# Two transformer layers on one core: row addresses by transposes, pinned engine orders and VectorE additions in the last stage

## The chip, the cores and the metric

The kernel runs on one core of one Trainium2 chip. The metric is the time of one execution in device microseconds (us), as the median of several runs; lower is better. Each profiled execution also has a span, from the first to the last instruction of the core, and the clock that TensorE was granted (1.00 is full speed, 0.50 half). The engines are named as in the profile: PE is TensorE's matmul and PEld its weight load, DVE is VectorE, ACT is ScalarE, POOL is GpSimd, and SP is the engine whose queue issues most DMAs.

## What is computed

Four sequences of 1024 tokens with 256 features pass through two layers, each an attention and a feed-forward part with residual additions. The change touches only the last of the four parts, a routed feed-forward layer in which each of 8 experts picks its best 128 tokens of a sequence:

```python
def _L1_ffn_ref(x, gate_w, experts):
    SINKHORN_ITERS = 8
    ...
    B, N, D = x.shape          # 4, 1024, 256
    E = gate_w.shape[-1]       # 8
    M = N // E                 # 128
    gate_logits = jnp.einsum('bnd,de->bne', x, gate_w)
    competitive_gates = sinkhorn(gate_logits)
    vals, idx = jax.lax.top_k(jnp.swapaxes(competitive_gates, -1, -2), M)
    gate_values = jnp.swapaxes(vals, -1, -2)
    routed_indices = jnp.swapaxes(idx, -1, -2)
    b_idx = jnp.arange(B)[:, None, None]
    routed = x[b_idx, routed_indices]
    routed = jnp.transpose(routed, (2, 0, 1, 3))
    outputs = jnp.einsum('ebmd,edf->ebmf', routed, experts)
    outputs = outputs * jnp.transpose(gate_values, (2, 0, 1))[..., None]
    vals_bmed = jnp.transpose(outputs, (1, 2, 0, 3))
    routed_back = jnp.zeros_like(x).at[b_idx, routed_indices].set(vals_bmed)
    return routed_back
...
x = x + _L1_ffn_ref(_layernorm(x, axis=-1), L1_ffn_gate_w, L1_ffn_experts)
return x
```

Where two experts pick the same token, the later expert's value stands (`set`). So each token gets at most one row of results, that of the highest expert that picked it, and a token picked by none gets zeros.

## The kernel before

The tokens lie as 32 tiles `x_t[i]` of 128 tokens by 256 features; a sequence `b` has `TB` = 8 tiles. The sequences are treated in two groups, `SEQS`: group 0 is sequences 0 to 2, group 1 is sequence 3 alone, since its attention ends last. The code is written as Python generators that emit instructions; a scheduler then orders the instructions of each engine by its own estimate of when each is ready, unless an edge (`tc.issue_after`) pins one behind another. A list `in_turn`, when it is not empty, makes `mm_on` and `turn_on` (matmul and transpose on TensorE, line 82) keep program order; plain `mm` and `nc.tensor.transpose` don't. In the last stage `in_turn` is empty before the change.

The work of the last stage, which lies from about 2085 us to the end:

1. **Column and row sums of the gates** (`share_steps`, lines 1293 to 1324): eight rounds, each a sum over tokens on VectorE (L1305), a product with ones on TensorE (L82) and five short VectorE instructions (L1314 to L1321). Group 0's rounds run in the attention stage; group 1's eight rounds run here.
2. **The choice of tokens** (`choose_parts`): the gates of a group, by expert, are laid out as rows of 1024 tokens; sixteen times VectorE takes the eight largest of each row (`max`) and strikes them out (`match_replace`), all recorded at L1363. After that it looks for their indices (`max_index`, four for each half). Products on TensorE then lay out gate, token and row number of each slot: `slot_gate` (L1410, ScalarE), `slot_tok` and `slot_row` (L1408 and L1409, VectorE). For group 1 this is done in two parts, each after eight rounds. The generator yields between the VectorE instructions, and what is emitted between two yields is what may lie beside them. Inside `choose_parts` these VectorE instructions are already chained to one another.
3. **Gathering the chosen tokens** (`take_rows`, L1420): POOL issues one indirect DMA for each expert and sequence, 128 rows of 1 KB from the DRAM copy `xn_d` into a tile `xg`: 24 for group 0, and four for each part of group 1.
4. **The experts** (`experts_on`, `half_experts`): two tiles at a time are transposed on TensorE (L1436), copied to `xgT` by ScalarE (L1438), multiplied with two experts' weights (L1453, or L1490 for the half tiles of group 1), scaled by the gates on ScalarE into `yg` (L1463, L1499; four buffers) and stored by SP into the DRAM tile `y_d[b]` (L1467, L1503). `experts_on` transposes pair m ahead of the product of pair m - 1.
5. **Signs and ranks** (`signs`, L2133 and L2135): to find out which row of `y_d` belongs to a token, ScalarE makes for each expert a matrix of signs, token number (`place`, a ramp along the columns) against the slot's token (`half_less`), and TensorE multiplies it with a column of slot numbers (`whole_col`, `half_col`). What is accumulated in PSUM (`rank0`, `rank1`) is, for each expert and token, a sum that jumps from one token to the next by the slot's number where the expert has chosen that token. ScalarE copies the sums out (`sums_to`, L2178; `last_sums`, L2241).
6. **Row addresses** (`sources`, L2152 to L2162): for each of the eight tiles, three accumulated products turn the sums of one sequence into a key of 8 numbers per token: expert number, plus 8 times the sum shifted by one token, minus 8 times the sum. VectorE takes the largest of the eight (L2162): the row of `y_d` to be read, or a row of zeros.
7. **Back to the tokens** (`back`, L1511): POOL issues one indirect DMA per tile that reads the 128 rows and **adds** them into `x_t[i]` as it writes (`compute_op=ALU.add`). Then SP stores the tile to the output (`put`, L1521).

In the last stage's body (lines 2165 to 2246) the generators are mixed by counts: sums of group 1 beside experts and signs of group 0, then the choice of group 1 beside the rest of them and beside the addresses of each sequence when its eighth sign is in; then the two halves of sequence 3. The `y_d` rows of a sequence must have landed before its eight reading DMAs are issued.

## Time and profile before

| what | us |
|---|---|
| median of 6 runs (lowest to highest) | 2250.4 (2245.86 to 2258.06) |
| the profiled execution, its own time | 2250.11 |
| its span | 2248.4 |
| PE busy over the span | 2088.1 (93%) |
| DVE, ACT, POOL busy over the span | 1326.9, 1029.1, 641.2 |
| mean granted clock of TensorE over the span | 0.965 |
| group 1's first sum over tokens (L1305) starts | 2089.80 |
| group 1's first `max` (L1363) starts | 2134.64 |
| `slot_row` of group 1's second part ready | 2210.10 |
| last adding gather (L1511) starts | 2241.74 |

The times of the lower rows are microseconds from the start of the span. A line of the timeline gives the start, the duration, the engine, the line of the kernel, the operation, the output and inputs by name (`two`, `acc`, `misc` and `one` are PSUM tiles), the shapes, and how many instructions were merged. In square brackets stands how long the engine was idle before, and what released it; "issue" means that nothing that the profile shows was waited for, and "remote" a signal that the profile can't assign to an instruction. Durations of PE are modelled at their ends, since matmuls are pipelined; a float32 matmul leaves two records.

### The profile page before, as it was taken

Reading aid. Unit: us, or ns where it says so; the run is one execution under the profiler, and the core shown is the slowest. Engines: PE = TensorE matmul, PEld = TensorE weight load, DVE = VectorE, ACT = ScalarE, POOL = GpSimd, SP = SyncE. Lnnn points to the kernel's source line nnn. Section 1 sums busy time; section 2 is a strip of 40 time slices with the busy share of each in tenths; the row PEclk is TensorE's granted clock in tenths of the full one; section 3 lists DMA queues with packets and bytes.
Section 4 is the critical chain, followed back from the end, with each engine's and each line's share of the span. In section 5 each row is a group of like instructions: output and inputs, shape, how many; then the busy total and the mean of one; then the engine's idle time right before and its main releaser. Section 6 shows DMA issues by size and latency. Waiting matters only on the chain. (4 is left out here: it accounts for less than half of the span.)

```text
span 2248.4 us, 50565 instructions
## 1 busy us (share of the span) xinstructions
PE 2088.1 (93%) x20098; PEld 1378.6 (61%) x20098; DVE 1326.9 (59%) x2626; ACT 1029.1 (46%) x1941; POOL 641.2 (29%) x832
## 2 busy tenths in 40 slices
PE   6999989999999999998999999999999999997693
PEld 4777765555788888864555555555555555553472
DVE  6676654522222222245887878778787877898353
ACT  3555542111122222221266666767676766666352
POOL 3656541342000000023421222221221303024454
PEclk9999999999999999999999999999999999997676
DMA  4111106113167667734353222131313131101345
GB/s 147 52 45 48 49 13 200 50 63 136 52 222 237 219 215 233 225 112 103 85 112 68 52 50 61 50 76 49 77 49 77 46 64 42 45 2 55 87 97 119
DMA packets 207303, 212.66 MB, mean 95 GB/s; under 512 B 87208, under 2 KB 167432, under 8 KB 207068
## 3 DMA queue, kind: packets, MB, share of 16 engines
q1 hardware_dynamic: 181788, 169.39, 26.7%
q0 software_dynamic: 14048, 29.67, 5.1%
q10 hardware_dynamic: 11232, 10.37, 1.3%
q8 instruction: 159, 2.61, 0.5%
q14 instruction: 76, 0.62, 0.1%
HBM read 140.64 MB, written 56.92 MB: 88 GB/s over the span
## 5 line engine op out<-in xcount | busy, mean ns | idle before, releaser
L1772 ACT ACTIVATE wide<-one 128x512 f32<-128x512 f32 x1024 | 529.3, 602 | 215.9 <-PE one L86 210.2
L1722 DVE TENSOR_REDUCE tops<-two 128x2 f32<-128x1024 f32 x268 | 326.0, 1218 | 88.0 <-PE two L86 82.2
L1725 DVE TENSOR_REDUCE tops<-one 128x1 f32<-128x512 f32 x488 | 313.4, 680 | 15.2 <-PE one L86 15.2
L86 PE MATMUL acc<-wide,v_t 128*32 128x256 f32 x4096 | 278.7, 389 | 2.6 <-ACT wide L1772 2.1
L86 PE MATMUL two<-xbT,w_t 128*128 128x256 f32 (+1 forms) x1280 | 253.6, 356 | 2.0 <-ACT xbT L1155 1.4
L86 PE MATMUL one<-q_st,k_st 64*128 64x512 f32 x1024 | 238.3, 450 | 2.7 <-ACT wide L1772 1.9
L86 PEld LDWEIGHTS two<-xbT,w_t 128*128 128x128 f32 x1280 | 221.5, 190 | 29.7 <-ACT xbT L1155 1.8
L1188 DVE SCALAR_TENSOR_TENSOR glu_b<-two,b_blk,act_b 128x256 f32<-128x256 f32 (+1 forms) x160 | 72.6, 454 | 244.8 <-ACT act_b L1181 244.8
L86 PE MATMUL one<-top_st,minus 64*128 64x512 f32 x1024 | 209.4, 396 | 0.0
L1181 ACT ACTIVATE act_b<-two,b_blk 128x256 f32<-128x256 f32 (+1 forms) x160 | 72.1, 451 | 295.3 <-PE two L86 136.1
L86 PE MATMUL one<-k_st,q_st 64*128 64x512 f32 x488 | 172.6, 451 | 27.1 <-ACT wide L1772 22.6
L86 PEld LDWEIGHTS acc<-wide,v_t 128*32 128x32 f32 x4096 | 107.7, 109 | 113.7 <-issue 62.4
L289 ACT ACTIVATE act<-two,bT 128x512 f32<-128x512 f32 x60 | 41.2, 687 | 264.9 <-PE two L82 259.4
L86 PEld LDWEIGHTS one<-q_st,k_st 64*128 64x128 f32 x1024 | 101.6, 186 | 92.7 <-ACT wide L1772 39.6
L86 PEld LDWEIGHTS one<-k_st,q_st 64*128 64x128 f32 x488 | 86.8, 184 | 104.9 <-ACT wide L1772 77.7
L86 PE MATMUL acc<-w_t,glu_b 128*128 128x256 f32 x552 | 125.6, 379 | 0.0
L1933 POOL DMA_INDIRECT yr<-ys_d,slot x64 | 61.9, 967 | 211.9 <-DMA ys_d<-yb 80.3
L82 PE MATMUL two<-wide,w_t 128*128 128x512 f32 x256 | 115.1, 603 | 5.6 <-DVE tops L1722 4.9
L1238 POOL TENSOR_TENSOR x<-x,sb_b 128x256 f32<-128x256 f32 x32 | 23.2, 726 | 336.5 <-DVE glu_b L1188 336.5
L619 POOL TENSOR_SCALAR_AFFINE_SELECT pT<-pT 64x512 f32<-64x512 f32 x128 | 84.2, 658 | 114.0 <-ACT pT L609 112.0
L86 PEld LDWEIGHTS acc<-w_t,glu_b 128*128 128x128 f32 x552 | 101.9, 190 | 12.3
L1827 POOL TENSOR_TENSOR y<-y,wide 128x256 f32<-128x256 f32 x32 | 23.3, 730 | 300.7 <-DVE y L1824 235.4
(396 smaller groups left out, 3445.2 us busy)
## 6 DMA issues: line engine op xcount, KB each, us to landing
w_t<-in_L_ffn_rw_dram SPq DMA_DIRECT2D x120, 512.0 KB
halves<-split SPq DMA_DIRECT2D x64, 256.0 KB
q_st<-halves SPq DMA_DIRECT2D x128, 128.0 KB
k_st<-halves SPq DMA_DIRECT2D x256, 64.0 KB
xb<-xs_d SPq DMA_DIRECT2D x31, 256.0 KB
ys_d<-yb ACTq DMA_DIRECT2D x31, 256.0 KB
xs_d<-zeros SPq DMA_DIRECT2D x5, 1536.0 KB
b_t<-in_L_ffn_rb_dram SPq DMA_DIRECT2D x40, 128.0 KB
```

The lines of the kernel that those rows point to most:

```text
L82: return do(*args, **kw)
L86: done = do(*args, **kw)
L289: nc.scalar.activation(act, ps[0], AF.Silu, bias=bT[0][:, f, e : e + 1])
L619: nc.gpsimd.affine_select(out=part, in_=part, compare_op=ALU.is_ge, fill=0.0, base=0, pattern=[[0, 8], [1, WIN]], channel_multiplier=-1,)
L1181: nc.scalar.activation(act[:, :cols], ps[:, ff * cols : (ff + 1) * cols], AF.Silu, bias=b_blk[0][:, f, n : n + 1],)
L1188: nc.vector.scalar_tensor_tensor(glu[:, f, :cols], ps[:, 512 + ff * cols : 512 + (ff + 1) * cols], b_blk[1][:, f, n : n + 1], act[:, :cols ...
L1238: nc.gpsimd.tensor_tensor(x_t[m], x_t[m], sb3_b, ALU.add).ins, newest_glu[0]
L1722: last = nc.vector.tensor_reduce(tops[:, :, j, kk], whole[0], AX.X, ALU.max)
L1725: last = nc.vector.tensor_reduce(tops[:, hh, j, kk : kk + 1], sc[hh], AX.X, ALU.max)
L1772: newest["scalar"] = nc.scalar.activation(pt[:, hh * 512 : (hh + 1) * 512], sc[hh], AF.Exp).ins
L1827: nc.gpsimd.tensor_tensor(y, y, bo_b, ALU.add)
L1933: ga = nc.gpsimd.indirect_dma_start(out=yr[:, :], out_offset=None, in_=ys_d[:, :], in_offset=bass.IndirectOffsetOnAxis(ap=slots[k][:, i : ...
```

## The change

- **Addresses.** The slot columns are scaled by `0.5 * E` instead of 0.5, and the first column of the sums holds minus (expert number plus a constant). Before the first sign of a sequence a product of `place` with `e_part` (expert number / 128 in all 128 rows, two matmuls of 512 columns in float32) adds a ramp of expert number times token number to the accumulated sums. The difference of the sums of two neighbouring tokens then is the whole key. `turned_sums` transposes the sums and the sums shifted by one (16 transposes of 8 by 128 into one PSUM bank), ScalarE copies the first half out (`before`), and VectorE subtracts (`key`) and takes the largest. The products of L2152 and L2154 go, and with them `times_e`.
- **Orders.** `in_line` pins every instruction that passes through it behind the last one of its engine: ScalarE's copies, signs and scalings, VectorE's choice, keys and addresses, and POOL's ramp, gathers and reads. `in_turn` is set, and all TensorE work of the stage goes through `mm_on` and `turn_on`. The body of the stage becomes a written-out order; a pair of experts is transposes, sign, product, sign, two sums, and three steps of the choice. Signs get six buffers. The place of each sum among the pairs is fixed by this order.
- **Additions.** For sequences 2 and 3 the reading DMA no longer adds; it writes a tile `yr`, and VectorE adds it to `x_t[i]`. The stores of sequences 2 and 3 come after the last stores of rows.
- **The tail.** Sequence 3's sums are copied out half by ScalarE and half by VectorE, and the order there is: signs, first transposes, copies of the sums, first pair, the 16 transposes of the sums, second pair, keys.

```diff
@@ -92,6 +92,17 @@
     def turn_on(*args, **kw):
         return on_tensor(nc.tensor.transpose, *args, **kw)
+    lines = {"scalar": [], "vector": [], "gpsimd": []}
+    def in_line(engine: str, do, *args, **kw):
+        with ExitStack() as behind:
+            for ins in lines[engine]:
+                behind.enter_context(tc.issue_after(ins))
+            done = do(*args, **kw)
+        lines[engine][:] = [done.ins]
+        return done
     const = ctx.enter_context(tc.tile_pool(name="const", bufs=1))
...
@@ -1433,9 +1439,9 @@
         for h, xg in enumerate(xgs):
             for kc in range(2):
                 c = (2 * h + kc) * P
-                nc.tensor.transpose(ps[:, c : c + P], xg[:, kc * P : (kc + 1) * P], ident)
+                turn_on(ps[:, c : c + P], xg[:, kc * P : (kc + 1) * P], ident)
         xgT = pool.tile([P, 4, P], F32, tag="xgT", name="xgT", bufs=3)
-        nc.scalar.copy(xgT.rearrange("p k t -> p (k t)"), ps)
+        in_line("scalar", nc.scalar.copy, xgT.rearrange("p k t -> p (k t)"), ps)
...
@@ -1446,48 +1452,39 @@
         slot_gate = chosen[g, 0][0]
-        def product(m: int, xgT):
+        for m in range(0, len(xgs), 2):
+            xgT = turned(xgs[m : m + 2], pool)
+            yield m
             ps = two_banks()
             for h in range(2):
                 for kc in range(2):
-                    mm(
+                    mm_on(
                         ps[:, h * D : (h + 1) * D],
                         lhsT=xgT[:, 2 * h + kc, :],
-                        rhs=w_all[:, (2 * m + h) % E, kc, :],
+                        rhs=w_all[:, (m + h) % E, kc, :],
                         start=(kc == 0),
                         stop=(kc == 1),
                     )
             for h in range(2):
-                b, e = divmod(2 * m + h, E)
+                b, e = divmod(m + h, E)
                 yg = pool.tile([P, D], F32, tag="yg", name="yg", bufs=4)
-                nc.scalar.activation(
+                in_line(
+                    "scalar", nc.scalar.activation,
                     yg, ps[:, h * D : (h + 1) * D], AF.Copy,
-                    scale=slot_gate[:, 2 * m + h : 2 * m + h + 1],
+                    scale=slot_gate[:, m + h : m + h + 1],
                 )
                 nc.sync.dma_start(out=slots_of(SEQS[g][b], e, 0, CAP), in_=yg)
...
             yield m
-    def half_experts(g: int, part: int, m: int, xgs, pool, w_all):
+    def half_experts(g: int, part: int, m: int, xgT, pool, w_all):
...
@@ -1505,16 +1503,22 @@
                     in_=yg[64 * h : 64 * h + 64, :],
                 ).ins
...
+    def backs(b: int, src_row, pool, adds: bool):
+        rows = []
+        for t in range(TB):
+            i = b * TB + t
+            yr = pool.tile([P, D], F32, tag="yr", name="yr", bufs=2 * TB) if adds else x_t[i]
+            in_line(
+                "gpsimd", nc.gpsimd.indirect_dma_start,
+                out=yr[:, :],
+                out_offset=None,
+                in_=y_d[b][:, :],
+                in_offset=bass.IndirectOffsetOnAxis(ap=src_row[:, t : t + 1], axis=0),
+                compute_op=ALU.bypass if adds else ALU.add,
+            )
...
-            whole_col.rearrange("p n e -> p (n e)")[:, :: E + 1], slot_i, 0.5, None, ALU.mult
+            whole_col.rearrange("p n e -> p (n e)")[:, :: E + 1], slot_i, 0.5 * E, None, ALU.mult
         )
         for h in range(2):
...
-        first_sum = -0.5 * (CAP * (CAP + 1) // 2)
+                    half_i[half, part, :], 0.5 * E, None, ALU.mult,
+                )
         n0 = len(SEQS[0])
         sums_to = wpool.tile([32 * (n0 - 1) + E, 1 + S], F32, name="sums_to")
-        nc.gpsimd.memset(sums_to[:, 0:1], first_sum)
         last_sums = wpool.tile([E, 1 + S], F32, name="last_sums")
-        nc.gpsimd.memset(last_sums[:, 0:1], first_sum)
+        e_i = wpool.tile([E, 1], I32, name="e_i")
+        nc.gpsimd.iota(e_i, pattern=[[0, 1]], base=E * CAP * (CAP + 1) // 4, channel_multiplier=1)
+        for rows in [sums_to[32 * b : 32 * b + E] for b in range(n0)] + [last_sums]:
+            nc.gpsimd.tensor_scalar(rows[:, 0:1], e_i, -1.0, None, ALU.mult)
+        e_part = wpool.tile([P, E], F32, name="e_part")
+        nc.gpsimd.tensor_scalar(e_part, expert_no[:, 0], 1.0 / P, None, ALU.mult)
         def half_less(g: int, part: int):
             tok = chosen[g, part][1]
...
@@ -2127,123 +2131,146 @@
             nc.vector.tensor_scalar(less, tok, -1.0, 0.5, ALU.mult, ALU.add)
             return less
...
+        def sign(less, n: int):
+            hot = pool.tile([P, S], BF16, tag="hot", name="hot", bufs=6)
+            in_line("scalar", nc.scalar.activation, hot, place, AF.Sign, bias=less[:, n : n + 1])
+            return hot
+        def halves_on(ps, lhsT, rhs, start: bool, stop: bool):
             for hf in range(2):
-                newest["ranks"] = mm(
+                newest["ranks"] = mm_on(
                     ps[:, hf * 512 : (hf + 1) * 512],
-                    lhsT=col,
-                    rhs=hot[:, hf * 512 : (hf + 1) * 512],
+                    lhsT=lhsT,
+                    rhs=rhs[:, hf * 512 : (hf + 1) * 512],
                     start=start,
                     stop=stop,
                 ).ins
-        def sources(rows, mine):
-
-
+        def turned_sums(rows, mine):
             ps = one_bank()
...
+            for n in range(2):
+                for t in range(TB):
+                    c = (n * TB + t) * E
+                    turn_on(
+                        ps[:, c : c + E], rows[:, t * P + n : (t + 1) * P + n], ident[mine, mine]
                     )
...
+            before = pool.tile([P, TB * E], F32, tag="before", name="before")
+            in_line("scalar", nc.scalar.copy, before, ps[:, : TB * E])
+            return ps, before
+        def sources(ps, before):
+            key = pool.tile([P, TB, E], F32, tag="key", name="key")
+            in_line(
+                "vector", nc.vector.tensor_tensor,
+                key.rearrange("p t e -> p (t e)"), ps[:, TB * E : 2 * TB * E], before, ALU.subtract
+            )
+            src_row = pool.tile([P, TB], I32, tag="src_row", name="src_row")
+            in_line("vector", nc.vector.tensor_reduce, src_row, key, AX.X, ALU.max)
             return src_row
+        in_turn.append("all")
         less0 = half_less(0, 0)
         xgs0 = take_rows(chosen[0, 0], [(n // E, n) for n in range(n0 * E)], pool)
         rank0 = two_banks()
...
+        jobs = experts_on(0, xgs0, pool, w_all)
+        hots, summed = [], iter(range(n0 * E))
+        def one_sign():
+            hots.append(sign(less0, len(hots)))
+        def sum_signs(n: int):
+            for _ in range(n):
+                n = next(summed)
                 b, e = divmod(n, E)
...
+                ps = rank0[32 * b : 32 * b + E]
+                if e == 0 and b:
+                    halves_on(ps, e_part, place, True, False)
+                halves_on(ps, whole_col[:, e, :], hots[n], False, e == E - 1)
+        def ranks(b: int):
             mine = slice(32 * b, 32 * b + E)
...
+            in_line("scalar", nc.scalar.copy, sums_to[mine, 1:], rank0[mine, :])
+            return turned_sums(sums_to[mine], mine)
+        halves_on(rank0[:E], e_part, place, True, False)
         for n, _ in enumerate(share_steps(1, one_bank, 0)):
+            next(jobs)
             if n:
...
+                sum_signs(1)
+            one_sign()
+        choose = choose_parts(1, one_bank, lambda: None, 2)
+        def go_on(n: int):
+            for _ in range(n):
+                next(choose, None)
+        def pair_of_experts():
+            next(jobs)
+            one_sign()
+            next(jobs)
+            one_sign()
+            sum_signs(2)
+            go_on(3)
+        go_on(3)
+        sum_signs(1)
+        at = ranks(0)
+        go_on(1)
+        for _ in range(2):
+            pair_of_experts()
+        backs(0, sources(*at), pool, False)
+        for _ in range(2):
+            pair_of_experts()
+        at = ranks(1)
+        pair_of_experts()
+        go_on(1)
+        backs(1, sources(*at), pool, False)
+        for _ in range(3):
+            pair_of_experts()
         put(0)
-        for _ in sign_job:
-            pass
-        columns = [(NB - 1, m) for m in range(E // 2)]
+        at = ranks(2)
+        while (1, 0) not in chosen:
+            go_on(1)
+        less = half_less(1, 0)
+        xgs = take_rows(chosen[1, 0], [(NB - 1, m) for m in range(E // 2)], pool)
         rank1 = two_banks()[:E]
...
+        halves_on(rank1, e_part, place, True, False)
+        def last_signs(part: int):
+            for m in range(E // 2):
+                halves_on(
+                    rank1, half_col[:, part, m, :], sign(less, m), False,
+                    part == 1 and m == E // 2 - 1,
+                )
+        go_on(6)
+        adds = backs(2, sources(*at), pool, True)
+        last_signs(0)
         for m in range(0, E // 2, 2):
...
+            half_experts(1, 0, m, turned(xgs[m : m + 2], pool), pool, w_all)
+            go_on(4)
+        with tc.issue_after(newest["outputs"]):
+            put(1)
+        while (1, 1) not in chosen:
+            go_on(1)
+        less = half_less(1, 1)
+        xgs = take_rows(chosen[1, 1], [(NB - 1, m) for m in range(E // 2)], pool)
+        last_signs(1)
+        xgT = turned(xgs[:2], pool)
+        half = S // 2
+        in_line("scalar", nc.scalar.copy, last_sums[:, 1 : 1 + half], rank1[:, :half])
+        nc.vector.tensor_copy(last_sums[:, 1 + half :], rank1[:, half:])
+        half_experts(1, 1, 0, xgT, pool, w_all)
+        at = turned_sums(last_sums, slice(0, E))
+        half_experts(1, 1, 2, turned(xgs[2:], pool), pool, w_all)
+        adds += backs(NB - 1, sources(*at), pool, True)
+        for x, yr in adds:
+            nc.vector.tensor_tensor(x, x, yr, ALU.add)
+        with tc.issue_after(newest["outputs"]):
+            for b in range(2, NB):
                 put(b)
...
```

## The prediction

> **What bounds the kernel now.** First the overall row and the clock: PE is 93% busy over the span, but the page's slices show that only the last ones, from about 2090 us, mix all engines; the change lies there, and before 2085 us nothing moves. Then the chain of waits and the timeline from 2090 us on. The first view is the timeline of VectorE's choice of tokens for the last sequence, which the end of the kernel hangs on:
>
> ```profile
> 2134.64 1.22 DVE L1363 MAX8 top_v<-cur 32x8 f32<-32x1024 f32 x1
> ...
> 2147.26 0.23 DVE L2162 TENSOR_REDUCE src_row<-misc 128x8 int32<-128x64 f32 x1 [6.28 <-PE misc L2154]
> ...
> 2167.72 0.23 DVE L2162 TENSOR_REDUCE src_row<-acc 128x8 int32<-128x64 f32 x1 [8.79 <-PE acc L2154]
> ...
> 2187.21 0.23 DVE L2162 TENSOR_REDUCE src_row<-misc 128x8 int32<-128x64 f32 x1 [8.59 <-PE misc L2154]
> ...
> 2209.93 0.17 DVE L1409 CAST slot_row<-slot_tok 128x4 int32<-128x4 f32 x1
> ```
>
> From the first maximum (2134.64) to the list of rows (2210.10) it takes 75.5 us, and 6.28 + 8.79 + 8.59 = 23.7 us of it VectorE stands still at a row-address reduction that came into its queue before TensorE had made its input. Behind it stand the next maxima, and behind those the last gathers. Second, the end, and what a gather costs without and with the addition:
>
> ```profile
> 2214.64 0.94 POOL L1420 DMA_INDIRECT xg<-xn_d,slot_row  x1 [0.30 <-issue]
> ...
> 2217.35 0.20 PEld L1436 LDWEIGHTS acc<-ident,xg 128*128 128x128 f32 x2 [0.94 <-DMA xg<-xn_d,slot_row]
> ...
> 2228.83 1.57 POOL L1511 DMA_INDIRECT x<-y_d,src_row  x1 [13.24 <-DVE src_row L2162]
> ...
> 2239.90 1.53 POOL L1511 DMA_INDIRECT x<-y_d,src_row  x1 [0.30 <-issue]
> 2241.74 1.54 POOL L1511 DMA_INDIRECT x<-y_d,src_row  x1 [0.30 <-issue]
> ```
>
> Eight adding gathers follow each other at 1.84 us, plain ones at 0.95 + 0.30 = 1.25; a plain one lands 2.7 us after its start. Third, an odd stretch in the column sums:
>
> ```profile
> 2112.61 0.21 DVE L1314 RECIPROCAL rc<-misc 128x8 f32<-128x8 f32 x1 [11.04 <-remote]
> ...
> 2120.29 0.59 ACT L1438 COPY xgT<-acc 128x512 f32<-128x512 f32 x1 [9.97 <-remote]
> ```
>
> VectorE and ScalarE wait there for products that TensorE shows as ended at 2103.1 and 2103.6. Nothing in the trace explains it. It ends at 2120.3, some 2 us after the last packet of the 24 gathers (2118). I call it the hold.
>
> **The change, part by part.** *Start.* The ramp (iota 1.02, cast 1.05) now comes ahead of all 24 gathers and after the last normalised tile (2085.7), with one store of 0.61 between: the first gather starts near 2088.6 instead of 2084.5, the second lands at 2089.9 + 2.7 = 2092.5, and TensorE, now in program order, holds its first transposes (2091.0 before) for it; behind them stand all later sums. Ahead of the first sum it also makes the ramp product: two matmuls, four records of 512 columns; the 256-column product of the same type has 0.216 us a record (1.73 over eight), so 4 x 0.43 = 1.7, or 3.4 at half clock. Start 2 to 3 us later; the gather stream ends 1.7 later. Two expert pairs leave the loop of sums, which makes it shorter, but the hold, if it stays, sets its end. I take +1.5 us at the first maximum, bounds -17 (no hold) and +4.
>
> *Row addresses.* Before, 24 products a sequence: on TensorE 7.0, 6.7, 9.5 and 6.4 us (2140.18 to 2147.15, and so on). After, 16 transposes; L1436 has four in 0.49 at full clock and 0.91 at half, so 1.9 or 3.6. Added: a ScalarE copy of 64 columns (0.2 to 0.3) and a subtraction on VectorE (0.23, as the 128x64 products). The ramp products add 1.7 to 3.4 for each of the other three sequences, but stand beside ScalarE's scaling and sign (1.9 us): 0.3 to 1.5 each. The smaller constants on POOL cost nothing: POOL idles 22.4 us before them.
>
> *Pinned order.* VectorE's 23.7 us go. What is late next is the pair of experts, for TensorE and ScalarE now strictly take transposes, copy, product, two scalings, sign, sum, and only then the next transposes. The rows of one pair before:
>
> ```profile
> 2126.78 0.65 PE L1436 MATMUL acc<-ident,xg 128*128 128x128 f32 x4
> ...
> 2127.27 1.89 PE L1453 MATMUL two<-wide,xgT 128*128 128x256 f32 x8
> ...
> 2127.50 0.57 ACT L1438 COPY xgT<-acc 128x512 f32<-128x512 f32 x1
> ...
> 2129.09 0.59 PE L2135 MATMUL two<-hot,whole_col 128*8 128x512 bf16 x2
> ...
> 2129.25 0.84 ACT L1463 ACTIVATE yg<-two,slot_gate 128x256 f32<-128x256 f32 x2 [1.19 <-issue]
> ...
> 2129.98 1.15 ACT L2133 ACTIVATE hot<-wide,half_less 128x1024 bf16<-128x1024 f32 x1
> ```
>
> Transposes to copy 0.72; copy to the product that needs it 0.64 (2120.29 to 2120.93); product to scaling 1.98; scaling to sign 0.73; sign to its sum 1.20 (2210.26 to 2211.46); sum to the next work 0.53 (2129.09 to 2129.62). Together 5.8 us a pair. VectorE gets three steps beside each, 3 x 1.28 = 3.85, so it outruns the pairs and waits for them at the address keys. From the first maximum: last sum, copy and 16 transposes 3.7; four pairs 23.2; copy and transposes 3.0; four pairs 23.2; copy, transposes, small copy, subtraction and reduction 4.0; then the ten microseconds of VectorE that come after that key (four steps 5.1, four index searches 4.85); lists 1.0 (2209.14 to 2210.10); ramp products 1. That is 69 at full clock.
>
> The clock. In the windows view (busy time of PE, its weight loads, VectorE, ScalarE and POOL, then the granted clock, then DMA) the clock falls to 0.50 in every address block:
>
> ```profile
> 2130.00:2135.00 5.00, 5.00 (x32) 3.64 (x31) 3.22 (x12) 3.72 (x7) 0.00 (x0) 1.00 0.31 105
> ...
> 2180.00:2185.00 5.00, 5.00 (x25) 5.00 (x25) 0.00 (x0) 1.94 (x2) 4.09 (x4) 0.50 0.56 86
> ```
>
> The second row lies inside the block of 9.5 us. At half clock a pair costs 0.5 more in its transposes, 1.7 in the product (3.62 at 2121.84 against 1.89) and 0.4 in its sum: 2.6. How many of the eight pairs run so, no row shows; between none (69) and all, with the blocks (95). I take about one and a half, 3.5 us, because the mix of products and sums ran at 1.00 before (2130 to 2140): 72.5, against 75.5. Gain 3.0.
>
> The Trainium skill, "TensorE: Matmul & The Clock Gate", section "HAM oscillation — how this bites in real kernels", has the clock halve only for idle gaps above some 3.4 us; by that no pair would pay and the stretch be an estimated 69. The same page's "Part 4: PE-mode transpose" says that transposes do not count as busy, which speaks against this change: by that every address block would still end cold, an estimated 3 x 2.6 on top, about 77.
>
> *Queues.* SP holds the scaled rows' stores and those of finished sequences; before, sequence 0's stores held the next store of rows from 2153.4 to 2163.4. A scaled row has four buffers, two pairs or 11.6 us, so ten such microseconds cost nothing; at a longer hold the excess falls on the pairs. On POOL the second scatter (8 x 1.84 = 14.7) starts about 31 after the first maximum and is through by 46, two before the next row list; the third (plain, 10.0) starts near 58 to 61 and is through one to four before the last list. Both at nothing; without that cover they would cost 14.7 and 10.
>
> *End.* Before, 38.3 us from the row list to the end (2210.10 to 2248.4). The four gathers, signs and sums stay (row list + 5.5). Then transposes, copy, first products (1.9), 16 transposes (1.9), second pair 0.7 + 0.6 + 2.0, two scalings, and four stores at 0.63: the last is issued near +16 and landed 2.1 later (2224.56 to 2226.7 before), so the first gather starts near +18.1 instead of +18.7: 0.6. Seven intervals of 1.25 instead of 1.84: 4.2. Landing 2.7 instead of 4.0 (2241.74 to the store at 2245.72): 1.3. The addition on VectorE costs 0.55: no 128x256 addition from SBUF is in this stretch, bounds 0.25 (128x64) and 0.75 (POOL's 0.73). The second scatter's eight additions and the eight stores of sequence 2, moved here, lie beside those ten microseconds of gathers; without that cover 8 x 0.6 = 5. Gain 5.5, less 0.5 for a cold product: 5.0.
>
> **Sum:** 2250.1 + 1.5 - 3.0 - 5.0 = 2243.6, so **2243**. The profiled execution's 2250.11 stands 0.3 under the median of the six runs, 2250.4; span and what lies around it differ by 1.7.
>
> **The rivals.**
> *Pinned chain at half clock (slower).* Place: the eight pairs after the loop of sums. Price 2.6 a pair and 1.7 a block. Against the forecast's one and a half, four pairs bring it back to the time before (6.5 / 2.6 = 2.5 more), six or more make it clearly slower: all but one with two blocks is 2243 + 5.5 x 2.6 + 2 x 1.7, about 2260. For it: TensorE now idles 0.6 and 1.9 us in every pair, and the clock was down to 0.80 from 2175 to 2180, where TensorE had only a few sums to do. Against it: 0.93 and 1.00 from 2150 to 2160.
> *The hold goes too (faster).* If it came from that order of work, two rounds of sums take 4.9 us by the rows above, eight with two cold microseconds 21.4, from 2092.6 to 2114 instead of 2131: 17 us earlier than I took, 2226. For it: no explanation ties it to the gathers. Against: six runs within 12 us, so it is steady, and the gathers remain.
> *The change frees nothing.* The keys wait as long as before, and the last gathers for stores instead of addresses: 2250. For it: the last stores land at 2226.7 before, two microseconds ahead of the first gather; against: the gathers' interval, which falls anyway.
>
> **How the numbers follow.** This kernel's measurement tells 0.3%, 6.8 us, from no change. Forecast 0.46 (its own range 2236 to 2254; nearly half of it beyond -0.3%): faster 0.23, same 0.21, slower 0.02. Half clock 0.24, all slower. No hold 0.24, all faster. Frees nothing 0.06, same. Together faster 0.47, same 0.27, slower 0.26. To leave out two in ten the range runs from the no-hold time to just past the half-clock one: 2226 to 2261.
>
> **What would show it.** Right: src_row without long waits except for the third, where VectorE waits some 7 us; pairs 5.8 us apart; the last eight gathers at 1.25 us from some 18 us after the row list. Wrong: pairs at 8 us and a clock of 0.5 through 2140 to 2190; the first maximum before 2125 (no hold) or after 2141; additions that lag the landings.

## The result and the profile after

The changed kernel takes 2256.63 us (median of 24 runs, 2248.95 to 2261.82), the kernel before 2252.55 us (53 runs): a ratio of 1.0018, 95% interval 1.001 to 1.0026. The forecast was 2243, 0.3% less; the change does not gain at all. The profiled execution took 2258.97 us, its span is 2257.3. Set beside the span before (2248.4) that is 8.9 us more, in three places:

| stretch of the last stage | before | after | forecast |
|---|---|---|---|
| first sum to first maximum | 44.8 | 47.2 | 1.5 more |
| first maximum to last row list ("the choice") | 75.5 | 79.1 | 3.0 less |
| last row list to the first of the last gathers | 18.7 | 24.6 | 0.6 less, 0.5 more for a cold product |
| from there to the end | 19.6 | 15.6 | 4.95 less |

The rest, 1.0, was there at the first sum already (2090.78 against 2089.80); in the eighteen profiles of this study that start lies anywhere from 2086.7 to 2098.5, so kernels are compared below by stretches of their stage and by ratios of their runs.

VectorE's choice, from the timeline (start, duration, engine, line, operation; in brackets the idle time before and its releaser; line 103 is the helper that pins orders):

```profile
2137.95 1.22 DVE L103 MAX8 top_v<-cur 32x8 f32<-32x1024 f32 x1
...
2170.07 0.23 DVE L103 TENSOR_TENSOR key<-misc,before 128x64 f32<-128x64 f32 x1 [9.99 <-ACT before L103]
...
2191.42 0.16 DVE L1414 COPY slot_tok<-misc 128x4 f32<-128x4 f32 x1 [5.53 <-PE misc L86]
...
2202.11 0.23 DVE L103 TENSOR_TENSOR key<-misc,before 128x64 f32<-128x64 f32 x1 [7.75 <-ACT before L103]
...
2216.92 0.16 DVE L1415 CAST slot_row<-slot_tok 128x4 int32<-128x4 f32 x1
```

The wait at the first address is gone. But 9.99 + 5.53 + 7.75 = 23.3 us stand at the second, at the first row list and at the third: as much as the 23.7 before. The 3.7 us by which the choice is longer are mostly work of VectorE's own: it is busy 52.9 us of it instead of 50.1, since six of the additions of sequence 2 stand in it. What VectorE waits for has changed. It was address products that came late; now it is the pairs of experts, behind which the sums, and so the keys, stand. One pair in the timeline of TensorE and ScalarE, with the product of the next pair, which comes behind an address block, as its last line:

```profile
2161.20 0.66 PE L86 MATMUL acc<-ident,xg 128*128 128x128 f32 x4
...
2161.90 0.58 ACT L103 COPY xgT<-acc 128x512 f32<-128x512 f32 x1 [1.27 <-PE acc L86]
...
2162.53 1.99 PE L86 MATMUL two<-wide,xgT 128*128 128x256 f32 x8 [0.68 <-ACT xgT L103]
...
2164.46 0.59 PE L86 MATMUL two<-hot,whole_col 128*8 128x512 bf16 x2
...
2166.54 0.59 PE L86 MATMUL two<-hot,whole_col 128*8 128x512 bf16 x2 [1.49 <-ACT hot L103]
...
2171.51 3.78 PE L86 MATMUL two<-wide,xgT 128*128 128x256 f32 x8 [0.68 <-ACT xgT L103]
```

Everything in a pair waits for the step before it, and TensorE idles 0.68 and 1.49 us. The product takes 1.99 us in one pair and 3.78 in the other. Of the eight products five take 3.3 to 3.8; a product at half clock is called cold from here on. Two rows of the windows view (busy time of PE, its weight loads, VectorE, ScalarE, POOL, then the granted clock, DMA share, GB/s) say why, and two more for the end:

```profile
2150.00:2155.00 5.00, 2.84 (x15) 1.34 (x13) 4.86 (x7) 2.64 (x6) 4.09 (x4) 1.00 0.70 135
2155.00:2160.00 5.00, 4.19 (x10) 2.67 (x11) 4.89 (x6) 2.23 (x4) 4.39 (x3) 0.66 0.82 150
2215.00:2220.00 5.00, 2.60 (x32) 1.17 (x29) 1.43 (x7) 3.69 (x6) 1.87 (x2) 0.99 0.33 79
2220.00:2225.00 5.00, 3.85 (x13) 1.54 (x13) 0.31 (x1) 2.51 (x4) 1.93 (x3) 0.50 0.84 262
```

After five microseconds in which TensorE was busy for 2.84 and 2.60 us, the next five run at a lower clock. Windows that begin where the clock changes show it more sharply. From 2151.63 to 2155.04 TensorE is busy 1.25 of 3.41 us, and the clock goes to 0.50. From 2155.04 to 2158.46 the slow pair fills all 3.42, and it goes back to 1.00. The next 3.41 us, with 1.91 busy, leave it there, and from 2165.28 to 2168.70, with 1.07 of 3.42, it is lost again. Behind the last row list it falls to 0.50 at 2220 and stays there:

```profile
2224.24 3.68 PE L86 MATMUL two<-wide,xgT 128*64 128x256 f32 x16 [0.68 <-ACT xgT L103]
...
2231.44 3.68 PE L86 MATMUL two<-wide,xgT 128*64 128x256 f32 x16 [0.68 <-ACT xgT L103]
...
2241.71 0.95 POOL L103 DMA_INDIRECT yr<-y_d,src_row  x1 [19.17 <-DMA out_dram<-x]
...
2250.51 0.95 POOL L103 DMA_INDIRECT yr<-y_d,src_row  x1 [0.31 <-issue]
...
2254.12 0.43 DVE L2270 TENSOR_TENSOR x<-x,yr 128x256 f32<-128x256 f32 x1 [0.81 <-DMA yr<-y_d,src_row]
```

The releaser named at the first gather (a store to the output) is only the event that came nearest. The last store of rows is issued at 2237.44 and has landed at 2239.57, and the gather's record starts 2.14 us later. Before, it was the same: landed 2226.69, gather 2228.83. The row addresses, which the view names there, were ready at 2227.92; the first two adding gathers of that kernel start 0.26 and 0.27 us after theirs, this one 0.9. From there the gathers follow each other at 1.26 us instead of 1.84.

### The profile page after: what moved, and what is told of

It reads as the page before. It is cut to its first block, busy times and chain, and to the rows that moved or that the text cites. A ratio compares the mean times of both kernels' runs of the same rounds, so it can differ in the third digit from the quotient of the medians.

```text
span 2257.3 us, 50364 instructions
## 1 busy us (share of the span) xinstructions
PE 2083.0 (92%) x19986; PEld 1359.5 (60%) x19986; DVE 1333.3 (59%) x2647; ACT 1029.4 (46%) x1945; POOL 630.9 (28%) x834
## 5 line engine op out<-in xcount | busy, mean ns | idle before, releaser
L1729 DVE TENSOR_REDUCE tops<-one 128x1 f32<-128x512 f32 x488 | 313.3, 680 | 15.7 <-PE one L86 15.6
L1831 POOL TENSOR_TENSOR y<-y,wide 128x256 f32<-128x256 f32 x32 | 23.3, 731 | 302.5 <-DVE y L1828 248.3
```

Of the source, the lines that this page charges most:

```text
L1729: last = nc.vector.tensor_reduce(tops[:, hh, j, kk : kk + 1], sc[hh], AX.X, ALU.max)
L1831: nc.gpsimd.tensor_tensor(y, y, bo_b, ALU.add)
```

## Experiments

All ratios are to the kernel before on the same chip. The sets ran on several chips, which turned out to matter.

**Additions (e1, e10).** In e1 the gathers of the changed kernel add again:

```diff
-        adds = backs(2, sources(*at), pool, True)
+        backs(2, sources(*at), pool, False)
...
-        adds += backs(NB - 1, sources(*at), pool, True)
-        for x, yr in adds:
-            nc.vector.tensor_tensor(x, x, yr, ALU.add)
+        backs(NB - 1, sources(*at), pool, False)
```

> The changed kernel with its sixteen reading DMAs of sequences 2 and 3 adding again, VectorE's additions gone. If the interval of the gathers is what the additions bought (1.26 against 1.84 us, seven intervals, and an earlier landing, less 0.5 for the addition), the last gathers take about 19.6 us from the first to the end instead of 15.6, and the time is some 4 to 5 us above the changed kernel: about 2261. Rival: the additions were hidden in other work, or VectorE's own additions cost as much as they save: no difference, about 2256.

Ratio 1.003 (1.0016 to 1.0045), median 2257.2: less than the 2261 expected, and the interval overlaps that of the changed kernel. In the rows, from the first of the last gathers to the end it takes 19.5 us again. The third key to the last row list, though, falls from 14.6 to 13.3: VectorE's additions of sequence 2 did stand in the choice. e10 is the other way round, the kernel before with this part alone, and for sequence 3 only:

```diff
-            out=x_t[i][:, :],
+            out=yr[:, :],
...
-            compute_op=ALU.add,
+            compute_op=ALU.bypass if b == NB - 1 else ALU.add,
         )
+        if b == NB - 1:
+            nc.vector.tensor_tensor(x_t[i], x_t[i], yr, ALU.add)
```

> The kernel before with one part of the change alone: the eight reading DMAs of sequence 3 write a tile of their own and VectorE adds. By the change's own trace (1.26 against 1.84 us a gather, first gather to end 15.6 against 19.6 us): 4.0 us under the kernel before, ratio 0.998. Rival: VectorE's additions or their waits take it back: 1.000.

Ratio 0.998 (0.9968 to 0.9993), and 15.6 us from first gather to end. On the old order the additions gain what their rows said. On the new one only the rows show it, 3.9 us at the end less 1.3 in the choice; the whole times do not tell.

**Clock (e2, e3, e5, e13, e14).** Matmuls whose result is overwritten fill TensorE's gaps; the order of the real instructions stays. In the pairs and behind the last row list, as e14 has them:

```diff
+        def fill(ps, n: int):
+            for _ in range(2 * n):
+                mm_on(ps[:E, :256], lhsT=whole_col[:, 0, :], rhs=spare, start=True, stop=True)
...
-            sum_signs(2)
+            sum_signs(1)
+            if len(hots) < n0 * E:
+                filled.append(two_banks())
+                fill(filled[-1], 6)
+            sum_signs(1)
...
         xgT = turned(xgs[:2], pool)
+        fill(ps, 3)
```

> The changed kernel with matmuls of zeros put into TensorE's gaps behind the last row list, and nothing else. If the half clock of that stretch (0.50 from 2220 on) is what made it long, the clock stays at 1.00 there, the products take 1.95 instead of 3.68 us, and the first of the last gathers starts about 20 us behind the row list instead of 24.6: some 4.5 us less, about 2252. Rival: the stores of rows and their landing, or the order of work, set that start whatever the clock: no gain, or a loss of 1 to 2 us because the added matmuls stand ahead of the real ones.

> The changed kernel with matmuls of zeros in TensorE's gaps of the eight pairs (before each product and before each second sum) and before the transposed sums, nothing else. If five pairs at half clock cost 1.5 to 1.9 us each and the blocks 0.5, pairs come every 5.9 us throughout, the stretch from the first maximum to the last row list is about 70 instead of 79 us, and the time about 2248. Rival: the pairs are held by something else (stores of rows, ScalarE, signals that come late): the clock reads 1.00 and the stretch stays near 79, no gain.

Both had a tile of zeros of their own, which POOL clears. The stretches came out nearly as the clock theory had them: in e2 the first of the last gathers 19.9 us behind the row list, in e3 the choice 73.4 us instead of the 70 expected, with all eight products at 1.99. The whole times did not all follow: ratios 1.0035 (1.0022 to 1.0048), 6 us above what was expected, and 1.000 (0.9987 to 1.0012), 3.5 us above. In both profiles the stage's first sum came at 2098, 7 us later than after the change; POOL cleared the tile ahead of two normalised tiles, but how much of the 7 that makes was not tried, and profiles without such a tile have that sum as late as 2096.2 (e12). So the added matmuls were put on tiles that are there anyway, first at the end alone:

> The added matmuls behind the last row list again, now on tiles that are there anyway, so that nothing ahead of that list changes. Half clock as the cause: the first of the last gathers about 20 us behind the list as in the run before, and the whole time 4 to 5 us under the changed kernel, 2250 to 2252 (ratio to the kernel before about 1.000). Rival: the shorter end is real but the time comes out no lower, because something that the added work does to the stages before it takes it back: 1.002 or more.

0.9981 (0.9968 to 0.9994), first gather 19.2 us behind the list; but this chip gave 2234 us for the kernel before, and the changed kernel was not beside it. A single profile does not settle it either: without added matmuls in the pairs the choice took 75.8 us in e5 and e9, 79.5 in e2 and 81.6 in e13, with three to five of the eight products cold, and without any behind the list the first gather came between 19.5 (e9) and 24.6 us behind it. Then in both places, beside the changed kernel on one chip:

> The changed kernel once more, beside the next three on one chip: 0.9995 to 1.002 of the kernel before, and by its profile the clock behind the last row list is either up (first of the last gathers about 19.5 us behind the list) or down (24 to 25 us).

> The changed kernel with matmuls on idle tiles in TensorE's gaps of the pairs and behind the last row list, on tiles that are there anyway. If the clock is what the pinned pairs lost, pairs come every 5.9 us, the stretch from the first maximum to the last row list is 69 to 73 us instead of 76 to 79, the first of the last gathers 19 to 20 us behind the list in every execution, and the time 5 to 9 us under the changed kernel's. Rival: the serial chain itself holds it, whatever the clock: within 2 us of the changed kernel.

1.0027 (1.0014 to 1.0039) and 0.9983 (0.9973 to 0.9993); medians 2256.3 and 2247.77. The windows of ten microseconds, first the changed kernel's in e13:

```profile
2160.00:2170.00 10.00, 7.27 (x31) 5.18 (x32) 0.29 (x2) 4.23 (x7) 0.00 (x0) 0.68 0.36 101
2170.00:2180.00 10.00, 8.69 (x23) 3.68 (x21) 9.80 (x15) 4.11 (x7) 8.05 (x6) 0.64 0.46 79
```

and with the added matmuls:

```profile
2160.00:2170.00 10.00, 8.68 (x71) 6.02 (x71) 2.81 (x7) 5.34 (x9) 3.67 (x3) 1.00 0.72 170
2170.00:2180.00 10.00, 9.83 (x66) 6.21 (x64) 9.80 (x13) 6.48 (x10) 7.42 (x5) 1.00 0.44 78
```

The clock stands at 1.00 from 2140 to 2190, pairs come every 5.9 to 6.5 us outside the address blocks, all eight products take 1.99, the choice takes 70.6 us instead of 81.6, and the first gather comes 20.2 us behind the list instead of 21.9, which was neither of the two values expected. Work that computes nothing takes 8.5 us off the median. That is the half clock, shown.

**Order (e4, e12, e6).** e4 keeps the pins and writes out another order of a pair:

```diff
-            next(jobs)
-            one_sign()
-            next(jobs)
-            one_sign()
-            sum_signs(2)
+            ps = whole_product(m, xgT, w_all)
+            one_sign()
+            one_sign()
+            whole_rows(0, m, ps, pool)
+            at = None if b is None else ranks(b)
+            if m + 2 < n0 * E:
+                xgT = turned(xgs0[m + 2 : m + 4], pool)
+            sum_signs(2)
             go_on(3)
```

> The changed kernel with another written-out order of the eight pairs: product, then the transposes of the next pair, then the two sums; ScalarE signs during the product. No matmul is added. If it is the serial chain of a pair (transposes, copy, product, sign, sum one behind the other) that sets the stretch, a pair falls to about 3.7 to 4.2 us, the clock stays at 1.00 without fillers, VectorE waits less than 2 us at the keys, and the stretch from the first maximum to the last row list is 53 to 58 us instead of 79: about 2235. Rival: the queues behind it become the bound (POOL with 14.7 us for each of two adding scatters, SP with stores of finished sequences ahead of stores of rows): the stretch stays above 68, the time above 2245.

0.9926 (0.9912 to 0.9939), median 2233.24. In its timeline the pairs between two address blocks come every 3.45 us, with nothing added:

```profile
2143.06 1.99 PE L86 MATMUL two<-wide,xgT 128*128 128x256 f32 x8
...
2144.89 0.60 PE L86 MATMUL misc<-ident,xg 128*128 128x128 f32 x4
...
2146.51 1.99 PE L86 MATMUL two<-wide,xgT 128*128 128x256 f32 x8
...
2149.96 1.99 PE L86 MATMUL two<-wide,xgT 128*128 128x256 f32 x8
```

The choice takes 59.9 us, 19 less. By these profiles the order does 10.7 of it, the step from e14's 70.6, and the clock, which here stands at 1.00 from 2130 to 2180, does the rest. At the keys VectorE waits 0.9 us in all. The choice is a little longer than expected because VectorE still waits 3.7 us for the first row list and adds sequence 2 in between. Repeated on another chip:

> The kernel of e4 unaltered, for the comparison with e11 and e9 on one chip. Some 20 us under the changed kernel on any chip, as in e4; with all its gathers ahead of the sums, the first maximum 46 us behind the first sum where the hold is, 24 to 30 where it is not.

0.9903 (0.9881 to 0.9925), against 0.9995 for the changed kernel there (e9). e6 takes the pins of TensorE, ScalarE and POOL away, and those of VectorE's keys and addresses, and leaves their order to the scheduler; only the choice itself stays chained:

```diff
+        if engine != "vector":
+            return do(*args, **kw)
...
-        in_turn.append("all")
```

> The changed kernel with transposed addresses, additions and written-out order of emission, but with TensorE, ScalarE and POOL left to the scheduler (only VectorE's choice stays chained). If the pinned order made the serial pairs, the scheduler lets transposes of the next pair pass the second sum, pairs come under 5 us, VectorE's waits at the keys fall below 12 us in all, and the time is 5 to 15 us under the kernel before. Rival: the scheduler puts the keys too early again, as before the change, and VectorE's waits stay near 23 us: about 2246 to 2256.

0.9951 (0.9932 to 0.997), the choice 68.9 us, VectorE's waits for ScalarE's copy at the keys 1.9 and 4.3, and 5.4 for the DMA of an addition. Addresses and additions without the pins beat the kernel before clearly, which the change as made does on no chip (on a chip like this one 0.9995, e9 below): it was the pinned order that gave the gain back.

**The hold (e7, e9, e11, e15, e16).** The chip of e5 to e8 showed no hold: ScalarE and VectorE waited for no ended product in the sums. So did the next one:

> The changed kernel unaltered, beside the next three on one chip, since the last set ran on a chip on which the kernel before took 2234 instead of 2251 us and showed no hold in the column sums. If what the change loses lies in the pairs and behind the last row list, its ratio to the kernel before is 1.002 on any chip; if a part of it lies in the sums, it differs where the hold is missing.

0.9995 (0.9982 to 1.0007). The kernel before takes 2234.0 us there instead of 2251 to 2253. From first sum to first maximum the changed kernel needs 24.1 us there (47.2 with the hold), the old sums, in e10, 27.1 (44.8). So without the hold the changed loop of sums, two pairs shorter, gains 3 us; with it, it loses 2.3. The eight profiles of these two chips have no wait of ScalarE or VectorE with "remote" as its releaser in the last stage; the ten others all have one of 11 us or more. What makes the hold was tried by keeping 16 of the 24 gathers back until the sums are through:

```diff
+        xgs0 += take_rows(
+            chosen[0, 0], [(n // E, n) for n in range(E, n0 * E)], pool, newest["gates"]
+        )
```

> The kernel with the next pair's transposes ahead of the sums (2233), with 8 of the 24 gathers ahead of the column sums and the other 16 held until the sums are through. If the hold (ScalarE and VectorE waiting 15 us for products of TensorE that had ended) lasts as long as POOL issues plain gathers, it ends some 20 us earlier: the first maximum near 2118 instead of 2135, the time near 2220. If it belongs to this place in the sums and not to the gathers, the first maximum stays near 2135 and the time does not fall; the 16 late gathers may then cost up to 5 us in the pairs.

> As e7, beside the same kernel with all 24 gathers ahead (next run), on one chip. On a chip with the hold, and if plain gathers make it: the first maximum about 24 us behind the first sum instead of 46, the time 8 to 12 us under the next run's. If the hold does not depend on the gathers: no sooner than 44 us. On a chip without the hold it can only lose, since pairs wait for gathers: 5 to 10 us above the next run.

Both ran where there is no hold and could only lose: 0.9956 (0.9941 to 0.9971) and 0.9955 (0.9938 to 0.9972), the second 12.2 us above e12, more than was expected. The last set met a chip with the hold:

> The kernel of e8 with fewer added matmuls between row list and first sum and a row of them ahead of it: the first of the last gathers 18 to 18.7 us behind the list instead of 20.0, the time 1 to 2 us under e8's ratio of 0.988. Rival: no better, 0.988.

> As e15, with 16 of the 24 gathers held until the column sums are through. On a chip with the hold, and if plain gathers make it: the first maximum about 25 us behind the first sum instead of 46 and the time 8 to 15 us under e15's. If the hold does not depend on them: first maximum as in e15. On a chip without it: 6 to 12 us above e15's, since pairs wait for gathers.

0.9926 (0.9912 to 0.9939) and 0.9879 (0.9862 to 0.9897). First maximum 46.7 and 27.1 us behind the first sum, the second near the 25 expected if the gathers make it, and the medians 10.9 us apart. In e15, all gathers ahead (the last gather, then ScalarE's and VectorE's waits):

```profile
2123.42 0.96 POOL L103 DMA_INDIRECT xg<-xn_d,slot_row  x1 [0.30 <-issue]
...
2127.53 0.84 ACT L103 ACTIVATE yg<-two,slot_gate 128x256 f32<-128x256 f32 x2 [18.05 <-remote]
...
2128.29 0.21 DVE L1325 RECIPROCAL rc<-acc 128x8 f32<-128x8 f32 x1 [14.00 <-remote]
```

and in e16:

```profile
2114.63 1.22 DVE L103 MAX8 top_v<-cur 32x8 f32<-32x1024 f32 x1
...
2130.83 0.96 POOL L103 DMA_INDIRECT xg<-xn_d,slot_row  x1 [0.30 <-issue]
...
2134.67 0.21 ACT L103 COPY before<-misc 128x64 f32<-128x64 f32 x1 [11.92 <-remote]
2134.91 0.23 DVE L103 TENSOR_TENSOR key<-misc,before 128x64 f32<-128x64 f32 x1 [15.20 <-ACT before L103]
```

The sums are free, and the hold has moved with the late gathers into the pairs. In both kernels it ends about 3 us after POOL's last gather (2124.38 to 2127.53, 2131.79 to 2134.67). So on some chips a long row of plain gathers goes with waits of ScalarE and VectorE for work that TensorE shows as ended, and moving the row moves the waits. How the gathers hold the signals, and why there and not elsewhere, is open; each chip ran one set, so chip and hour are not told apart.

**A version that beats both (e8, e15).** e4's order, and besides: eight buffers for scaled rows, sequence 0's stores behind them, added matmuls behind the last row list, both last products ahead of the transposed sums, and the additions of sequence 2 behind the choice:

```diff
+        with tc.issue_after(newest["rows"]):
+            put(0)
...
-        at = turned_sums(last_sums, slice(0, E))
-        half_experts(1, 1, 2, turned(xgs[2:], pool), pool, w_all)
+        half_experts(1, 1, 2, xgT, pool, w_all, ps)
+        at = turned_sums(last_sums, slice(0, E))
...
-            nc.vector.tensor_tensor(x, x, yr, ALU.add)
+            in_line("vector", nc.vector.tensor_tensor, x, x, yr, ALU.add)
```

> The kernel with the next pair's transposes ahead of the sums, and besides: eight buffers for scaled rows and stores of sequence 0 behind the last of them, added matmuls behind the last row list, both last products ahead of the transposed sums, and VectorE's additions of sequence 2 behind the choice. Clock and order as causes: the choice 55 to 58 us instead of 59.9, the first of the last gathers 18.5 us behind the row list instead of 19.8, the time 2227 to 2231. Rival: the end is set by something else than TensorE (row stores at 0.6 us each): 19.8 as before, the time 2231 to 2234.

0.9879 (0.9863 to 0.9895) without the hold, median 2207.6: the choice takes 56.6 us, within the 55 to 58 expected, of which VectorE is busy 51.0 and waits 4.0 (3.6 of them at the first row list). The first gather came no earlier (20.0): the added matmuls met a cold clock (0.50 from 2165 to 2170), and the first sum began 2.9 us behind the list. With fewer of them (e15) that was 1.9, and the gather came after 19.2; expected were 18 to 18.7. Where the hold is, e16's late gathers are the better ones.

## Why the prediction was wrong

The likeliest case failed; of the rivals, "pinned chain at half clock" named the right mechanism, and the time lies between the two.

- **Start.** 2.3 us more in the sums instead of 1.5 (1.4 to 2.4 over the six profiles of this loop with the hold and all gathers ahead of it); the ramp product took 3.42, its half-clock price. That the hold would stay and set the loop's end was right, and e16 fits the reason given, that the gathers remain.
- **Row addresses.** Right, and cheaper than said: 16 transposes take 1.16 to 1.87 us. Nothing of the loss lies here.
- **Pinned order.** The serial pair at full clock was priced at 5.8 us and measured 5.86; the stretch at 69 us, measured 70.6 where the clock is held (e14). Where VectorE waits was not right: the sign given was the third key alone, some 7 us, and even with the clock held it waits 7.1 us at the second key, 1.9 at the first row list and 5.7 at the third.
- **The clock: the step that failed.** "I take about one and a half, 3.5 us": five of eight pairs ran cold, at 1.5 to 2.0 us each and not 2.6, and every address block ended cold. The term measures 79.1 - 70.6 = 8.5 us in the first profile and 11.0 in e13 against e14; with three cold pairs, in e5 and e9, it is 5.2, which leaves the choice at 75.8, no shorter than before. The reason given, that the mix of products and sums ran at 1.00 before, compared two different mixes: before, the scheduler filled the gaps of one pair with the work of another (PE busy 5.00 of 5.00 from 2130 to 2135). Pinned, the same work leaves 2.84 of 5.00 from 2150 to 2155, and the clock falls.
- **The Trainium skill** ("TensorE: Matmul & The Clock Gate"). By "HAM oscillation — how this bites in real kernels" the rule is to leave no idle gaps above some 3.4 us; here the clock fell at 2155 with no gap above 1.5 us since 2149, so to keep that rule is not enough. The other one, "Part 4: PE-mode transpose", gave an estimated 77 us and was nearer: after each block of 16 transposes the next work ran cold (products of 3.53 and 3.78 us, a ramp product of 3.58). But its reason is not shown. With matmuls added ahead of the first two blocks (e14) the products behind them took 1.99, and so did those behind the first two blocks of e4, where nothing was added; and before the change the clock fell in a block of address products, which are no transposes, with TensorE busy for all of the 3.41 us ahead (2140.50 to 2143.91).
- **Queues.** As said: the second scatter was through before the next row list, the third 4 us before the last.
- **End.** The gathers' part was right: forecast 4.95 (4.2 + 1.3 - 0.55), measured 4.0. The part ahead of them was wrong twice. The clock: "less 0.5 for a cold product", but the stretch ran cold from 2220 on; with it held, the first gather comes 4.4 to 5.5 us earlier (e14, e5). And a term was left out: the sum let the gather start when the last store has landed (18.1), although before it started 2.1 us later (2226.69 to 2228.83). With both, 18.1 + 2.1 + 4.4 = 24.6. Three profiles of the changed kernel gave 19.5, 21.9 and 24.6: the clock of their five-microsecond windows behind the list was 0.82 or more in e9 (2190 to 2205), came back late in e13 and stayed at 0.50 in the first.
- **Additions at nothing.** Nearly: 1.3 us of sequence 2's additions stood in the choice.
- **The sum.** It gives 2243.6, which the text writes as 2243. The terms as measured in the first profile, 0.8 more at the start, 5.0 for the clock and 1.6 for the stretch at full clock, 6.0 ahead of the last gathers and 1.0 behind, make 2258.0 of it; the profiled execution took 2258.97, of which 1.0 was there before the stage.

## What to carry to other kernels

Pinning an order fixes not only who goes first but also every gap; write it so that TensorE's next independent work (here the next pair's transposes) stands ahead of whatever waits for another engine, and read the result from pairs of rows: interval, idle before, granted clock. A stall is not removed when its cause is made cheaper, but when the chain behind it is: sum the waits of the engine that bounds the stage before and after. When the clock wavers, a stretch has two prices, and matmuls that compute nothing, put in its gaps, tell the clock from the chain.

## What the runs showed of the hardware that was not expected

- The same kernel is 17 us faster on some chips: with the hold 2251 to 2253 us, without it 2234. The hold follows plain gathers and ends 2.9 us (e16) to 3.9 us (e14) after the last one; beside adding gathers (1.84 us apart) the pairs of e4 showed none, but after its eight plain gathers of sequence 2 ScalarE waited 6.3 us (to 2194.27).
- The clock fell to half after 3.41 us in which TensorE was busy for 1.25, without a gap above 1.5 us, and came back after 3.42 us that a slow product filled; 1.91 busy of 3.41 were enough to keep it. With added matmuls, TensorE busy for 87% and more of every ten microseconds, it stayed at 1.00. The busy share alone does not decide: before the change it fell after 3.41 us that address products filled.
- The first of the last gathers starts 2.14 us after the last store that it waited for had landed, in the kernel before, in the changed one and in e14 alike; behind address lists of VectorE gathers started after 0.26 to 0.4 us.
